# A segmented recurrence with a gated FFN: from block 2 on, token tiles of 16 steps of one batch instead of 8 steps of both

## The chip, the cores and the metric

The kernel runs on one core of a Trainium2 chip. A core has TensorE (PE: matrix products; its weight loads are shown apart as PEld), VectorE (DVE), ScalarE (ACT), GpSimd (POOL), and SyncE (SP), which here only issues transfers; 16 DMA engines move data between HBM and the on-chip memory SBUF. Engines run their own instruction streams in order and wait for each other by semaphores. The metric is device microseconds of one launch, lower is better, as the median of several runs.

## The reference

Two layers over x of shape (2 batches, 1024 steps, 512), each with a layer norm before and after and a residual:

```python
u = einsum('bsd,hd->bsh', layernorm(x), W_in) + b_in          # 512 -> 1024
s[t] = tanh(u[t] + s[t-1] * gamma + beta)                     # over 1024 steps, per channel
x = x + layernorm(einsum('bsh,dh->bsd', s, W_out) + b_out)
h = layernorm(x)
f = silu((h @ fp8(gate_w)) * gate_scale) * ((h @ fp8(up_w)) * up_scale)     # 512 -> 1536
x = x + layernorm((f @ fp8(down_w)) * down_scale)
```

fp8() rounds a weight to 8-bit floating point; the products themselves are of float32 values.

## The kernel before, in words

**Tiling of the recurrence.** The 1024 steps of a batch are cut into G = 8 segments of L = 128 steps that run side by side: with B = 2 batches that is GB = 16 columns for each of NH = 8 groups of 128 hidden channels, so one step of the recurrence is an operation on 128 partitions x 128 columns. A segment starts from a state that a warm-up finds: before the main pass, the last WARM = 96 steps of every segment are run from an arbitrary start, and the state at their end becomes the start (s0) of the *next* segment. The last column of the 16, the last segment of batch 1, has no next segment, and the warm-up leaves it out: WB = 15 columns, 120 per step. (The last segment of batch 0 is also warmed up and its result not used.) At the end `verdict` compares the states that the main pass reached with those that the warm-up had found; if they differ, or a weight's sum isn't finite, `sequential` computes everything again; otherwise the last two output tiles are stored.

**Blocks and tiles.** The 128 steps of a segment are cut into NB = 8 blocks of K = 16 steps. A block has 256 tokens, in two tiles of 128 tokens: TT = 8 steps of all 16 columns, in the order (step, batch, segment). `x_tok` and `out_tok` give this order in HBM; a load or store of a tile has the access pattern 8 x 16 x 512 there, in rows of 2 KB. The u of a block lies in `us[k]`, shape [128, NH, 16 steps, 16 columns], and the states are written over it in place.

**First stage** (lines 265 to 365). The order of blocks is 2 to 7, then 0 and 1; the number in this order is n. For each block: load x (`load_x`, line 154; the first two tiles in halves over the SP and ACT queues), statistics and norm on VectorE (`stat` 192, `norm` 199), transposes on TensorE (`trans_x`, 130), copies out of PSUM (`copy_x` 211), eight u products (`mm_u` 218), and their evacuation with bias on ScalarE (`evac_u` 227). The order on each engine is written out by hand. While the products of block n+1 run, the steps of block n run: `warm_step` for blocks 2 to 7 (n < 6), `main_step` for blocks 0 and 1. A warm-up step is coef x state (L246), + u (L247), both on VectorE, and a tanh on ScalarE (L249); a main step is L260, L261 and L262. Between them VectorE does one filler operation per step: norm, statistics, a copy, or the expansion of a quantized weight (L183). The last warm step copies its state into s0, one copy per batch (L255).

**Second stage** (lines 369 on). For a tile of 128 tokens, `mm_y` (L384) multiplies the states with W_out, then come the layer norm and residual (`y_in`, `y_resid`, `y_norm`), transposes, the gate and up products (`mm_g`, L433), silu and product (`gate`, `f_in`), the down product (`down`, L462), the layer norm and the store (`o_in`, `o_stat`, `o_out`). The loop runs over blocks k and 12 chunks fc of the FFN's inner width. While block k is in the FFN, the y products of block k+1 run at fc = 1 and fc = 4, and the 16 main steps of block k+2 are dealt out over the fc by the table STEPS. `load_r` (line 376) loads x again for the residual, behind the stores on the SP queue. `verdict` (lines 497 to 515) is called once at k = 6, fc = 7: a memset (L501), a comparison per batch (L505), reductions, a small matmul `pf` (L512), and the flag. The last two tiles' stores are the ones behind the flag's branch (L633).

Of the kernel before, what the change touches and what calls it, by code (L numbers as in the profile page):

```python
# [9 lines left out]
F32 = mybir.dt.float32  # L10
# [3 lines left out]
AF = mybir.ActivationFunctionType  # L14
ALU = mybir.AluOpType
AX = mybir.AxisListType
PSUM = bass.MemoryType.PSUM

P = 128
# [8 lines left out]
G = 8  # L28
# [4 lines left out]
def segmented(  # L33
# [21 lines left out]
    nc = tc.nc  # L55
    B, S, D = x.shape
    H = w_in.shape[1]
    I = gate_w.shape[1]
    ND, NH, NI = D // P, H // P, I // P
    L = S // G  # L60
    GB = G * B
    WB = GB - 1
    TT = P // GB
    K = 2 * TT
    N = K * GB
    NB = L // K

    x_tok = x.rearrange("b (g s) d -> s (b g) d", g=G)
    out_tok = out.rearrange("b (g s) d -> s (b g) d", g=G)

    const = ctx.enter_context(tc.tile_pool(name="const", bufs=1))
    weights = ctx.enter_context(tc.tile_pool(name="weights", bufs=1))
    states = ctx.enter_context(tc.tile_pool(name="states", bufs=1))
    small = ctx.enter_context(tc.tile_pool(name="small", bufs=4))
# [10 lines left out]
    hid = const.tile([P, 3, NH], F32, name="hid")  # L85
    ident = const.tile([P, P], F32, name="ident")
    mhalf = const.tile([P, 1], F32, name="mhalf")
    bias_u = const.tile([P, NH], F32, name="bias_u")
    coef = const.tile([P, NH, GB], F32, name="coef")
    coefw = const.tile([P, NH, WB], F32, name="coefw")  # L90
    ones = const.tile([P, 1], F32, name="ones")
    ffs = const.tile([P, 2, NI], F32, name="ffs")
    bout_bc = const.tile([P, D], F32, name="bout_bc")
# [13 lines left out]

    def constants_hid():
        nc.vector.tensor_tensor(bias_u, hid[:, 0, :], hid[:, 1, :], ALU.add)
        nc.vector.tensor_copy(coef, hid[:, 2, :].unsqueeze(2).broadcast_to([P, NH, GB]))  # L110
        nc.vector.tensor_copy(coefw, hid[:, 2, :].unsqueeze(2).broadcast_to([P, NH, WB]))


    def stats(src):
# [16 lines left out]

    us = {}

# [7 lines left out]
    order = list(range(first, NB)) + list(range(first))  # L144
    held = {}
    win_sb = win_p.tile([P, ND, H], F32, name="win_sb")

    def load_x(n, j, queues=(nc.sync,)):
        i = 2 * order[n] + j
        x_t = held["x", n, j] = xp.tile([P, D], F32, tag="x", name=f"x_{i}")  # L150
        w = D // len(queues)
        for h, queue in enumerate(queues):
            at = slice(h * w, (h + 1) * w)
            queue.dma_start(out=x_t[:, at], in_=x_tok[i * TT : (i + 1) * TT, :, at])

    def load_win(i):
        at = slice(i * H // 4, (i + 1) * H // 4)
# [54 lines left out]

    def mm_u(n, hc):
        if hc == 0:
            us[order[n]] = states.tile([P, NH, K, GB], F32, name=f"us_{n}")
        pu = held["u", n, hc] = ps_g.tile([P, 2, N], F32, tag="pg", name=f"pu_{n}_{hc}")
        for dc in range(ND):
            nc.tensor.matmul(  # L218
                pu[:, 0, :],
                lhsT=win_sb[:, dc, hc * P : (hc + 1) * P],  # L220
                rhs=held["xT", n][:, dc, :],
                start=(dc == 0),
                stop=(dc == ND - 1),
            )

    def evac_u(n, hc):
        nc.scalar.activation(  # L227
            us[order[n]][:, hc],
            held["u", n, hc][:, 0, :].rearrange("p (t q) -> p t q", t=K),
            AF.Identity,  # L230
            bias=bias_u[:, hc : hc + 1],
        )


    run = {"state": None}
    kept = []
    s0 = const.tile([P, NH, GB], F32, name="s0")
    nc.gpsimd.memset(s0.rearrange("p h (b g) -> p h b g", b=B)[:, :, :, 0], 0.0)

    def warm_step(k, t, last):  # L240
        z = small.tile([P, NH, WB], F32, tag="zw", name=f"zw_{k}_{t}", bufs=2)
        u = us[k][:, :, t, 0:WB]
        if run["state"] is None:
            z = u
        else:
            nc.vector.tensor_tensor(z, coefw, run["state"], ALU.mult)  # L246
            nc.vector.tensor_tensor(z, z, u, ALU.add)  # L247
        s = small.tile([P, NH, WB], F32, tag="sw", name=f"sw_{k}_{t}", bufs=2)
        nc.scalar.activation(s, z, AF.Tanh)  # L249
        run["state"] = s  # L250
        if last:

            for b in range(B):
                q = slice(b * G, (b + 1) * G - 1)
                nc.vector.tensor_copy(s0[:, :, b * G + 1 : (b + 1) * G], s[:, :, q])  # L255
            run["state"] = s0

    def main_step(k, t):
        z = small.tile([P, NH, GB], F32, tag="z", name=f"z_{k}_{t}", bufs=2)
        nc.vector.tensor_tensor(z, coef, run["state"], ALU.mult)  # L260
        nc.vector.tensor_tensor(z, z, us[k][:, :, t], ALU.add)  # L261
        nc.scalar.activation(us[k][:, :, t], z, AF.Tanh)  # L262
        run["state"] = us[k][:, :, t]

    def step(n, t):
        if n < WARM // K:
# [4 lines left out]

    both = (nc.sync, nc.scalar)
    load_x(0, 0, both)
    load_x(0, 1, both)
    nc.scalar.dma_start(out=hid, in_=per_hidden)
    nc.sync.dma_start(out=ffs, in_=per_ffn)
    load_win(0)
    load_win(1)
    load_x(1, 0)
    load_x(1, 1)  # L280
    load_win(2)
# [15 lines left out]
    for j in range(2):  # L297
        copy_x(0, j, 0, scalar=True)
        copy_x(0, j, 1)
    constants_hid()  # L300
    for j in range(2):
        for h in range(2):
            stat(1, j, h)
    for hc in range(NH):
        mm_u(0, hc)
        if hc in (4, 5):
            trans_x(1, hc - 4)
        if hc == 0:
            for j in range(2):
                for h in range(2):  # L310
                    norm(1, j, h)
        if hc in (5, 6):
            for h in range(2):
                copy_x(1, hc - 5, h)
        if hc == 6:
            for j in range(2):
                for h in range(2):
                    stat(2, j, h)
        evac_u(0, hc)
        if hc in (4, 5, 6):  # L320
            quant(hc - 4)
            expand(hc - 4)
            load_w(hc - 1)
# [7 lines left out]
    for n in range(NB - 1):  # L331
        mine = []
        for t in range(K):
# [26 lines left out]
            if n in (1, 2, 3, 4) and t == 9:  # L360
                c = slice((n - 1) * NH // 4, n * NH // 4)
# [11 lines left out]

    def load_r(i):
        held["x", i] = xr.tile([P, D], F32, tag="xr", name=f"xr_{i}")
        nc.sync.dma_start(out=held["x", i], in_=x_tok[i * TT : (i + 1) * TT])


    def mm_y(i, part=range(NH)):
        k, t0 = i // 2, (i % 2) * TT  # L380
        if part[0] == 0:
            held["py", i] = ps_y.tile([P, D], F32, tag="py", name=f"py_{i}")
        for hc in part:
            nc.tensor.matmul(  # L384
                held["py", i],
                lhsT=us[k][:, hc, t0 : t0 + TT, :].rearrange("p t q -> p (t q)"),
                rhs=wout_sb[:, hc, :],
                start=(hc == 0),
                stop=(hc == NH - 1),
            )  # L390
# [86 lines left out]
    def o_out(i):  # L477
        m, r = held["omr", i]
        o = held["o", i]
        c = small.tile([P, 1], F32, tag="cc", name=f"cc_{i}")  # L480
        nc.vector.scalar_tensor_tensor(c, m, r, held["c", i], ALU.mult, ALU.add)
        nc.vector.scalar_tensor_tensor(o, o, r, held["x", i], ALU.mult, ALU.add)
        nc.vector.tensor_scalar(o, o, c, None, ALU.subtract)
        dst = out_tok[i * TT : (i + 1) * TT]
        if i < 2 * NB - 2:
            nc.sync.dma_start(out=dst, in_=o)
        else:
            kept.append((dst, o))
# [8 lines left out]
    def verdict():  # L497


        bad = small.tile([P, NH, GB], F32, tag="bad", name="bad", bufs=1)  # L500
        nc.vector.memset(bad, 0.0)  # L501
        ends = us[NB - 1][:, :, K - 1, :]
        for b in range(B):
            q = slice(b * G, (b + 1) * G - 1)
            nc.vector.tensor_tensor(bad[:, :, q], ends[:, :, q], s0[:, :, b * G + 1 : (b + 1) * G], ALU.not_equal)  # L505
        bad2 = small.tile([P, 2], F32, tag="bad2", name="bad2", bufs=1)
        nc.vector.tensor_reduce(bad2[:, 0:1], bad, AX.XY, ALU.max)
        off = small.tile([P, n_sums], F32, tag="off", name="off", bufs=1)
        nc.vector.tensor_scalar(off, sums, 0.0, 0.0, ALU.mult, ALU.not_equal)
        nc.vector.tensor_reduce(bad2[:, 1:2], off, AX.X, ALU.max)  # L510
        pf = ps_t.tile([P, ND, P], F32, tag="pt", name="pf")
        nc.tensor.matmul(pf[0:1, 0, 0:2], lhsT=ones, rhs=bad2, start=True, stop=True)  # L512
        n = small.tile([1, 1], F32, tag="n", name="n", bufs=1)
        nc.vector.tensor_reduce(n, pf[0:1, 0, 0:2], AX.X, ALU.add)
        nc.vector.tensor_copy(flag, n)


    for i in range(4):
        load_r(i)
    for i in range(2):  # L520
        mm_y(i)
    n = NB - 1
# [22 lines left out]
    for i in range(last + 3):  # L545
        k, fc = divmod(i, NI)
        more = k + 1 < NB
        steps = iter(())
        if k + 2 < NB:
            t0 = sum(sum(STEPS.get(c, ())) for c in range(fc))  # L550
# [38 lines left out]
        ends = [2 * k - 2, 2 * k - 1] if k else []  # L589
# [12 lines left out]
        if more and fc == 1 and k:  # L602
            for j in range(2):
                load_r(2 * k + 2 + j)
# [396 lines left out]
```

## Time and profile before

| | |
|---|---|
| median of 3 runs | 543.51 us (543.43 to 544.18) |
| profiled execution | 543.2 us; its span in the trace 541.4 us |
| mean granted TensorE clock | 0.993 |
| busy: PE, PEld, DVE, ACT, POOL | 515.2, 408.6, 360.3, 225.4, 55.7 us |
| chain that ended last, by engine | PE 66%, DVE 19%, ACT 8%, issue 3%, DMA 1%, POOL 1% |
| first warm-up step | 28.54 us |
| copies into s0, end of the warm-up | 126.93 us |
| first y product of the second stage's chain | 161.69 us |
| last store issued | 535.40 us |

All times in the trace are microseconds from the start of the span, and nanoseconds where a mean of one instruction is given. "L218" is line 218 of the kernel. A group line reads: line, engine, operation, output<-inputs, shape, number | busy time, mean of one | idle time of the engine just ahead of these instructions, and what ended it. The chain that ended last is followed back from the last instruction, at each step to what released it; it shows which work set the end. A window row reads: stretch and length, then busy time and number of instructions of PE, PEld, DVE, ACT and POOL, the clock granted to TensorE, the mean busy share of the 16 DMA engines, and GB/s. A busy TensorE is not TensorE at its peak, since matmuls are pipelined.

### The profile page before, as it was taken

Reading aid. Unit: us, or ns where it says so; the run is one execution under the profiler, and the core shown is the slowest. Engines: PE = TensorE matmul, PEld = TensorE weight load, DVE = VectorE, ACT = ScalarE, POOL = GpSimd, SP = SyncE. Lnnn points to the kernel's source line nnn. Section 1 sums busy time; section 2 is a strip of 40 time slices with the busy share of each in tenths; the row PEclk is TensorE's granted clock in tenths of the full one; section 3 lists DMA queues with packets and bytes.
Section 4 is the critical chain, followed back from the end, with each engine's and each line's share of the span. In section 5 each row is a group of like instructions: output and inputs, shape, how many; then the busy total and the mean of one; then the engine's idle time right before and its main releaser. Section 6 shows DMA issues by size and latency. Waiting matters only on the chain.

```text
span 541.4 us, 8064 instructions
## 1 busy us (share of the span) xinstructions
PE 515.2 (95%) x2818; PEld 408.6 (75%) x2818; DVE 360.3 (67%) x1017; ACT 225.4 (42%) x590; POOL 55.7 (10%) x152
## 2 busy tenths in 40 slices
PE   3999999999999899999999999999999999999991
PEld 2888877776547787789669777966987796689990
DVE  3488888886675767765856775585677657364634
ACT  1366666665423453335225333522533351123330
POOL 1111110010011111110110111010101101110101
PEclk9999999999999999999999999999999999999997
DMA  7653545332000000200200020011002001100101
GB/s 185 181 187 110 159 153 156 118 89 87 21 1 2 0 1 0 79 2 0 46 32 1 2 78 1 1 31 49 0 2 79 1 1 28 50 1 1 41 1 44
DMA packets 15808, 27.36 MB, mean 51 GB/s; under 512 B 1424, under 2 KB 3984, under 8 KB 15760
## 3 DMA queue, kind: packets, MB, share of 16 engines
q1 hardware_dynamic: 15344, 26.49, 16.7%
q8 instruction: 24, 0.39, 0.3%
q10 hardware_dynamic: 416, 0.27, 0.2%
q14 instruction: 24, 0.20, 0.1%
HBM read 22.57 MB, written 4.19 MB: 49 GB/s over the span
## 4 chain that ended last, share of the span: by engine, by line
PE 66%; DVE 19%; ACT 8%; issue 3%; DMA 1%; POOL 1%; ACTq 0%; DVEq 0%; POOLq 0%
PE pg L433 30%; PE py L384 17%; PE pd L462 15%; DVE zw L247 5%; ACT sw L249 5%; DVE zw L246 5%; PE pu L218 3%; DVE z L261 2%; DVE z L260 2%; ACT us L262 2%; PE ph L130 1%; DMA x<-in_x_dram 1%; DVE st L116 1%; DVE st L192 1%; DVE mv L121 1%
## 5 line engine op out<-in xcount | busy, mean ns | idle before, releaser
L218 PE MATMUL pu<-xT,win_sb 128*128 128x256 f32 x512 | 123.2, 391 | 2.3 <-ACT xT L211 0.5
L218 PEld LDWEIGHTS pu<-xT,win_sb 128*128 128x128 f32 x512 | 95.1, 193 | 26.3 <-ACT us L227 13.8
L384 PE MATMUL py<-wout_sb,us 128*128 128x512 f32 x256 | 112.4, 592 | 1.0 <-DVE y L394 1.0
L433 PE MATMUL pg<-hT,gate_sb 128*128 128x256 f32 x384 | 100.6, 297 | 0.0
L433 PE MATMUL pg<-hL,gate_sb 128*128 128x256 f32 x384 | 93.9, 280 | 0.0
L433 PE MATMUL pg<-hL,up_sb 128*128 128x256 f32 x384 | 93.3, 279 | 0.0
L433 PE MATMUL pg<-hT,up_sb 128*128 128x256 f32 x384 | 93.2, 278 | 0.0
L447 DVE SCALAR_TENSOR_TENSOR f<-pg,ffs,gate 128x256 f32<-128x256 f32 x96 | 46.1, 481 | 68.2 <-ACT gate L443 68.2
L384 PEld LDWEIGHTS py<-wout_sb,us 128*128 128x128 f32 x256 | 48.4, 190 | 56.4 <-issue 54.1
L262 ACT ACTIVATE us<-z 128x128 f32<-128x128 f32 x128 | 39.7, 310 | 101.4 <-DVE z L261 99.1
L462 PE MATMUL pd<-down_sb,fL 128*128 128x512 f32 x192 | 75.9, 395 | 1.9 <-DVE fL L455 1.8
L433 PEld LDWEIGHTS pg<-hT,gate_sb 128*128 128x128 f32 x384 | 72.4, 189 | 6.1 <-issue 3.1
L433 PEld LDWEIGHTS pg<-hL,gate_sb 128*128 128x128 f32 x384 | 72.3, 188 | 5.8 <-issue 2.9
L462 PE MATMUL pd<-down_sb,fH 128*128 128x512 f32 x192 | 76.1, 396 | 0.0
L451 ACT CAST fH<-f 128x256 fp32r<-128x256 f32 x96 | 39.0, 407 | 80.7 <-DVE f L447 80.1
L433 PEld LDWEIGHTS pg<-hT,up_sb 128*128 128x128 f32 x384 | 72.5, 189 | 0.0
L433 PEld LDWEIGHTS pg<-hL,up_sb 128*128 128x128 f32 x384 | 72.3, 188 | 0.0
L443 ACT ACTIVATE gate<-pg,ffs 128x256 f32<-128x256 f32 x96 | 44.9, 468 | 59.8 <-PE pg L433 55.5
L123 POOL TENSOR_SCALAR var<-mv 128x1 f32<-128x1 f32 x64 | 14.2, 223 | 471.1 <-DVE mv L121 470.3
L455 DVE TENSOR_TENSOR fL<-f,fH 128x256 fp32r<-128x256 f32 x96 | 40.2, 418 | 10.9 <-ACT fH L451 10.3
L260 DVE TENSOR_TENSOR z<-coef,us 128x128 f32<-128x128 f32 x127 | 36.3, 286 | 12.2 <-ACT us L262 12.0
L249 ACT ACTIVATE sw<-zw 128x120 f32<-128x120 f32 x95 | 28.8, 303 | 34.4 <-DVE zw L247 34.3
(69 smaller groups left out, 508.8 us busy)
## 6 DMA issues: line engine op xcount, KB each, us to landing
xr<-in_x_dram SPq DMA_DIRECT2D x16, 256.0 KB
out_dram<-o SPq DMA_DIRECT2D x16, 256.0 KB
x<-in_x_dram SPq DMA_DIRECT2D x14, 256.0 KB
ws<-in_gate_w_dram SPq DMA_DIRECT2D x12, 256.0 KB
ws<-in_up_w_dram SPq DMA_DIRECT2D x12, 256.0 KB
ws<-in_down_w_dram SPq DMA_DIRECT2D x12, 256.0 KB
win_sb<-in_w_in_dram SPq DMA_DIRECT2D x4, 512.0 KB
wout_sb<-in_w_out_dram SPq DMA_DIRECT2D x4, 512.0 KB
```

The source lines that it names most:

```text
L218: nc.tensor.matmul(pu[:, 0, :], lhsT=win_sb[:, dc, hc * P : (hc + 1) * P], rhs=held["xT", n][:, dc, :], start=(dc == 0), stop=(dc == ND - 1),)
L246: nc.vector.tensor_tensor(z, coefw, run["state"], ALU.mult)
L249: nc.scalar.activation(s, z, AF.Tanh)
L260: nc.vector.tensor_tensor(z, coef, run["state"], ALU.mult)
L262: nc.scalar.activation(us[k][:, :, t], z, AF.Tanh)
L384: nc.tensor.matmul(held["py", i], lhsT=us[k][:, hc, t0 : t0 + TT, :].rearrange("p t q -> p (t q)"), rhs=wout_sb[:, hc, :], start=(hc == 0) ...
L433: nc.tensor.matmul(pg[:, n, :], lhsT=w[:, dc, fc * P : (fc + 1) * P], rhs=held[part, k][:, dc, :], start=(dc == 0 and part == "hT"), stop= ...
L443: nc.scalar.activation(g, held["g", i][:, 0, :], AF.Silu, scale=ffs[:, 0, i % NI : i % NI + 1])
L447: nc.vector.scalar_tensor_tensor(f, held["g", i][:, 1, :], ffs[:, 1, i % NI : i % NI + 1], held["gate", i], ALU.mult, ALU.mult)
L451: nc.scalar.copy(fH, f)
L455: nc.vector.tensor_tensor(fL, held["f", i], held["fH", i].bitcast(F32), ALU.subtract)
L462: nc.tensor.matmul(held["d", 2 * k + j], lhsT=held[part, i][:, j * P : (j + 1) * P], rhs=down_sb[:, fc, :], start=(fc == 0 and part == "fH ...
```

## The change

Blocks 0 and 1 stay as they are (`halved(k)`). In blocks 2 to 7 a tile is all 16 steps of the block of one batch: tile j is batch j, in the order (step, segment). The access pattern in HBM is then 16 x 8 x 512, again in rows of 2 KB. `us[k]` of these blocks is [128, NH, B, K, G], so that a tile's 128 tokens still lie side by side for the y product (`of_tile`), and a step (`at_step`) is 16 runs of 8 columns where it was 8 runs of 16. A y product of these blocks reads states of all 16 steps of the block; before, tile 0 read the first 8 and tile 1 the last 8.

The warm-up leaves out the last segment of each batch: WG = 7 segments, 2 x 7 x 8 = 112 columns per step instead of 120. The copy into s0 becomes one instruction instead of two; in the verdict a memset and two comparisons become one comparison. The constants, the scratch tiles and the step functions take the shape [128, NH, B, G or WG]. The instructions and their order on every engine are otherwise the same; in the compiled program the transposes of x and the first two y products wait for one more event of TensorE's own.

```diff
-    WB = GB - 1
+    WG = G - 1
...
-    x_tok = x.rearrange("b (g s) d -> s (b g) d", g=G)
-    out_tok = out.rearrange("b (g s) d -> s (b g) d", g=G)
+    def halved(k):
+        return k < 2
+    def tokens(t, i):
+        k, j = divmod(i, 2)
+        if halved(k):
+            return t.rearrange("b (g s) d -> s (b g) d", g=G)[i * TT : (i + 1) * TT]
+        return t[j].rearrange("(g s) d -> s g d", g=G)[k * K : (k + 1) * K]
...
+    def at_step(k, t):
+        return us[k][:, :, t] if halved(k) else us[k][:, :, :, t]
+    def of_tile(i, hc):
+        k, j = divmod(i, 2)
+        if halved(k):
+            return us[k][:, hc, j * TT : (j + 1) * TT].rearrange("p t b g -> p (t b g)")
+        return us[k][:, hc, j].rearrange("p t g -> p (t g)")
...
-            queue.dma_start(out=x_t[:, at], in_=x_tok[i * TT : (i + 1) * TT, :, at])
+            queue.dma_start(out=x_t[:, at], in_=tokens(x, i)[:, :, at])
...
-            us[order[n]] = states.tile([P, NH, K, GB], F32, name=f"us_{n}")
+            k = order[n]
+            us[k] = states.tile([P, NH, K, B, G] if halved(k) else [P, NH, B, K, G], F32, name=f"us_{n}")
...
     def warm_step(k, t, last):
-        z = small.tile([P, NH, WB], F32, tag="zw", name=f"zw_{k}_{t}", bufs=2)
-        u = us[k][:, :, t, 0:WB]
+        z = small.tile([P, NH, B, WG], F32, tag="zw", name=f"zw_{k}_{t}", bufs=2)
+        u = at_step(k, t)[:, :, :, 0:WG]
...
         if last:
-            for b in range(B):
-                q = slice(b * G, (b + 1) * G - 1)
-                nc.vector.tensor_copy(s0[:, :, b * G + 1 : (b + 1) * G], s[:, :, q])
+            nc.vector.tensor_copy(s0[:, :, :, 1:G], s)
             run["state"] = s0
...
     def main_step(k, t):
-        z = small.tile([P, NH, GB], F32, tag="z", name=f"z_{k}_{t}", bufs=2)
+        z = small.tile([P, NH, B, G], F32, tag="z", name=f"z_{k}_{t}", bufs=2)
         nc.vector.tensor_tensor(z, coef, run["state"], ALU.mult)
-        nc.vector.tensor_tensor(z, z, us[k][:, :, t], ALU.add)
-        nc.scalar.activation(us[k][:, :, t], z, AF.Tanh)
-        run["state"] = us[k][:, :, t]
+        u = run["state"] = at_step(k, t)
+        nc.vector.tensor_tensor(z, z, u, ALU.add)
+        nc.scalar.activation(u, z, AF.Tanh)
...
-        nc.sync.dma_start(out=held["x", i], in_=x_tok[i * TT : (i + 1) * TT])
+        nc.sync.dma_start(out=held["x", i], in_=tokens(x, i))
...
-                lhsT=us[k][:, hc, t0 : t0 + TT, :].rearrange("p t q -> p (t q)"),
+                lhsT=of_tile(i, hc),
...
-        dst = out_tok[i * TT : (i + 1) * TT]
+        dst = tokens(out, i)
...
     def verdict():
-        bad = small.tile([P, NH, GB], F32, tag="bad", name="bad", bufs=1)
-        nc.vector.memset(bad, 0.0)
-        ends = us[NB - 1][:, :, K - 1, :]
-        for b in range(B):
-            q = slice(b * G, (b + 1) * G - 1)
-            nc.vector.tensor_tensor(bad[:, :, q], ends[:, :, q], s0[:, :, b * G + 1 : (b + 1) * G], ALU.not_equal)
+        bad = small.tile([P, NH, B, WG], F32, tag="bad", name="bad", bufs=1)
+        nc.vector.tensor_tensor(bad, at_step(NB - 1, K - 1)[:, :, :, 0:WG], s0[:, :, :, 1:G], ALU.not_equal)
```

More of the change, by code (lines that the diff above doesn't have):

```diff
@@ L88, in segmented @@
     bias_u = const.tile([P, NH], F32, name="bias_u")
-    coef = const.tile([P, NH, GB], F32, name="coef")
-    coefw = const.tile([P, NH, WB], F32, name="coefw")
+    coef = const.tile([P, NH, B, G], F32, name="coef")
+    coefw = const.tile([P, NH, B, WG], F32, name="coefw")
     ones = const.tile([P, 1], F32, name="ones")
@@ L109, in constants_hid @@
         nc.vector.tensor_tensor(bias_u, hid[:, 0, :], hid[:, 1, :], ALU.add)
-        nc.vector.tensor_copy(coef, hid[:, 2, :].unsqueeze(2).broadcast_to([P, NH, GB]))
-        nc.vector.tensor_copy(coefw, hid[:, 2, :].unsqueeze(2).broadcast_to([P, NH, WB]))
+        for c in (coef, coefw):
+            c = c.rearrange("p h b g -> p h (b g)")
+            nc.vector.tensor_copy(c, hid[:, 2, :].unsqueeze(2).broadcast_to(c.shape))
     def stats(src):
@@ L227, in evac_u @@
         nc.scalar.activation(
-            us[order[n]][:, hc],
-            held["u", n, hc][:, 0, :].rearrange("p (t q) -> p t q", t=K),
+            us[order[n]][:, hc].rearrange("p a b g -> p (a b g)"),
+            held["u", n, hc][:, 0, :],
             AF.Identity,
@@ L236, in segmented @@
     kept = []
-    s0 = const.tile([P, NH, GB], F32, name="s0")
-    nc.gpsimd.memset(s0.rearrange("p h (b g) -> p h b g", b=B)[:, :, :, 0], 0.0)
+    s0 = const.tile([P, NH, B, G], F32, name="s0")
+    nc.gpsimd.memset(s0[:, :, :, 0], 0.0)
     def warm_step(k, t, last):
-        z = small.tile([P, NH, WB], F32, tag="zw", name=f"zw_{k}_{t}", bufs=2)
-        u = us[k][:, :, t, 0:WB]
+        z = small.tile([P, NH, B, WG], F32, tag="zw", name=f"zw_{k}_{t}", bufs=2)
+        u = at_step(k, t)[:, :, :, 0:WG]
         if run["state"] is None:
@@ L247, in warm_step @@
             nc.vector.tensor_tensor(z, z, u, ALU.add)
-        s = small.tile([P, NH, WB], F32, tag="sw", name=f"sw_{k}_{t}", bufs=2)
+        s = small.tile([P, NH, B, WG], F32, tag="sw", name=f"sw_{k}_{t}", bufs=2)
         nc.scalar.activation(s, z, AF.Tanh)
@@ L375, in load_r @@
         held["x", i] = xr.tile([P, D], F32, tag="xr", name=f"xr_{i}")
-        nc.sync.dma_start(out=held["x", i], in_=x_tok[i * TT : (i + 1) * TT])
+        nc.sync.dma_start(out=held["x", i], in_=tokens(x, i))
     def mm_y(i, part=range(NH)):
-        k, t0 = i // 2, (i % 2) * TT
         if part[0] == 0:
@@ L497, in verdict @@
     def verdict():
-        bad = small.tile([P, NH, GB], F32, tag="bad", name="bad", bufs=1)
-        nc.vector.memset(bad, 0.0)
-        ends = us[NB - 1][:, :, K - 1, :]
-        for b in range(B):
-            q = slice(b * G, (b + 1) * G - 1)
-            nc.vector.tensor_tensor(bad[:, :, q], ends[:, :, q], s0[:, :, b * G + 1 : (b + 1) * G], ALU.not_equal)
+        bad = small.tile([P, NH, B, WG], F32, tag="bad", name="bad", bufs=1)
+        nc.vector.tensor_tensor(bad, at_step(NB - 1, K - 1)[:, :, :, 0:WG], s0[:, :, :, 1:G], ALU.not_equal)
         bad2 = small.tile([P, 2], F32, tag="bad2", name="bad2", bufs=1)
-        nc.vector.tensor_reduce(bad2[:, 0:1], bad, AX.XY, ALU.max)
+        nc.vector.tensor_reduce(bad2[:, 0:1], bad.rearrange("p h b g -> p (h b g)"), AX.X, ALU.max)
         off = small.tile([P, n_sums], F32, tag="off", name="off", bufs=1)
```

## The prediction

> **What bounds the kernel now.** I read the chain of work that ended last first. Over the whole span it is two thirds TensorE, but cut into windows it shows four stages with four limits. To 28.5 us it goes through one load of x, its layer norm, and then TensorE alone:
>
> ```profile
> 1.97 5.01 DMA x<-in_x_dram
> 7.00 0.44 DVE st L192
> ...
> 8.72 0.42 DVE x L199
> 9.15 0.04 issue
> 9.19 1.13 PE px L130 x4
> 10.34 0.38 ACT xT L211
> 10.73 0.04 issue
> 10.77 11.17 PE pu L218 x40
> ```
>
> (start, duration, what). Every microsecond by which that load lands sooner moves TensorE's start, until the chain in front of it is bound elsewhere. From 28.54 to 126.93 us the chain is only the warm-up recurrence, 96 steps of two VectorE operations (L246, L247) and one tanh (L249): 98.4 us, 1.03 us a step. Beside them TensorE looks full, but it spends 11.5 us waiting for ScalarE to empty PSUM, so it is not the limit. Blocks 0 and 1 follow with the same recurrence 128 columns wide, and from about 190 us on TensorE runs without a gap to 530 us. Last come the final layer norm and two stores, whose data moves from about 535 to 540 us.
>
> The groups of instructions, with shapes kept apart (busy us, mean ns of one), price a step:
>
> ```profile
> L262 ACT ACTIVATE us<-z 128x128 f32<-128x128 f32 x128 | 39.7, 310 | 101.4 <-DVE z L261 99.1
> L261 DVE TENSOR_TENSOR z<-z,us 128x128 f32<-128x128 f32 x128 | 37.5, 293 | 4.5
> L260 DVE TENSOR_TENSOR z<-coef,us 128x128 f32<-128x128 f32 x127 | 36.3, 286 | 12.2 <-ACT us L262 12.0
> L249 ACT ACTIVATE sw<-zw 128x120 f32<-128x120 f32 x95 | 28.8, 303 | 34.4 <-DVE zw L247 34.3
> L247 DVE TENSOR_TENSOR zw<-zw,us 128x120 f32<-128x120 f32 x95 | 26.9, 283 | 3.6
> L246 DVE TENSOR_TENSOR zw<-coefw,sw 128x120 f32<-128x120 f32 x95 | 26.4, 278 | 8.7 <-ACT sw L249 1.3
> L505 DVE TENSOR_TENSOR bad<-us,s 128x56 f32<-128x56 f32 x2 | 0.3, 214 | 0.0
> ```
>
> The windows of busy time show at the head a stretch in which only loads of x are left, and near the end the two stores (the two columns before the last are the granted clock and the DMA engines' busy share; the last is GB/s):
>
> ```profile
> 16.00:17.00 1.00, 1.00 (x6) 0.90 (x5) 0.97 (x5) 0.20 (x1) 0.12 (x1) 1.00 1.02 348
> 19.00:20.00 1.00, 1.00 (x6) 0.90 (x5) 0.00 (x0) 0.00 (x0) 0.00 (x0) 1.00 0.53 170
> 536.00:537.00 1.00, 0.00 (x0) 0.00 (x0) 0.00 (x0) 0.00 (x0) 0.00 (x0) 0.50 0.42 113
> 537.00:538.00 1.00, 0.00 (x0) 0.00 (x0) 0.00 (x0) 0.00 (x0) 0.00 (x0) 0.50 0.49 156
> 538.00:539.00 1.00, 0.00 (x0) 0.00 (x0) 0.00 (x0) 0.00 (x0) 0.00 (x0) 0.50 0.46 139
> ```
>
> At 19 us and in the tail the share stops near one half, at 16 us, where weights load too, it reaches 1.02 at twice the rate.
>
> **The warm-up steps, 120 to 112 columns.** From 128 to 120 columns the rows fall by 286-278 = 8, 293-283 = 10 and 310-303 = 7 ns, 25 ns for eight columns. The change takes away eight more, and all three operations lie on the path. Against it: the operand u of L247 is now cut into 16 runs of 7 words, where it had 8 runs of 15. The Trainium skill (Vector Engine (DVE) Microarchitecture Reference, "Measured stream behaviour on trn2") states that a port keeps full rate only on adjacent pairs of words that start on an 8-byte boundary, and that an isolated word costs about 0.65 cycle. An odd run ends in one such word, so by the rule (my estimate) eight more of them cost 8 x 0.68 = 5.4 ns a step. The row beside it is L505: 56 columns in 8 runs of 7 on all three operands took 214 ns; a line through the 8-column bias_u add (156 ns) and the 128-column L260 (286 ns) puts 56 columns at 208, so 6 ns for 8 runs. The row doesn't contradict the rule, and it excludes a price several times higher. By rows alone I would gain 25 ns, with the rule 20; I take 21. Ten steps hold a bn_stats and bn_aggr pair, where VectorE and not the tanh is late; they gain about the VectorE part, 13 to 18. Sum: 95 x 21 ns = 2.0 us, bounds 1.1 (double the rule's price for the runs, and nothing on the ten steps) and 2.4. Next late in an ordinary step would be the filler operation on VectorE (norm, copy or expand, 0.41 us): it ends some 0.07 us before the tanh and gets earlier together with it, so it doesn't take over.
>
> **The handover and the verdict.** The two 56-column copies into s0 (188 ns each, 0.29 us together) become one of 112 columns, about 0.22: 0.1 gained, on the path. In the verdict a memset (0.15 us on the chain) and two comparisons (0.36) become one of 112 columns (about 0.27). That is 0.25 us, and TensorE is waiting for it:
>
> ```profile
> 482.39 0.19 PE L512 MATMUL pf<-bad,ones 128*1 128x2 f32 x2 [0.40 <-DVE bad L510]
> ```
>
> Its wait is 0.40 us, so all 0.25 count. Together 0.35 us, bounds 0.1 and 0.5.
>
> **Loads and stores.** The first load is block 2, which changes; so do the last two stores (block 7). Bytes and 2 KB rows stay; only the DRAM side's outer dimension goes from 8 to 16. The Trainium skill (DMA: Bandwidth & Descriptors, "Why a DMA increments its semaphore by 16 and not by 1") says that a transfer uses the largest number of engines up to 16 that divides the slowest dimension of both sides: 8 before, 16 after. The trace agrees in the shares of about 0.5. No row shows a 16-engine store of these bytes; a 16-engine mix of loads is the 348 GB/s row, against 170 GB/s with x alone. By the rule the moving halves; by the rows only what is not start-up and landing latency can halve.
>
> Head: 512 KB of x move in about 2.3 to 4.5 us, and the first tile lands at 4.98 (its first VectorE statistic), the second at 7.00. At double rate I put the first at about 4.2 and the second near 5. VectorE then needs two tiles of statistics, aggregates and the first norm: from the first landing to the second tile's norm about 3.0 us when nothing waits (0.75 + 0.25 + 0.75 + 0.25 to the second aggregate, then 1.05 as now from 7.67 to 8.72). That gives 7.2 to 7.5 in place of 8.72. I take 1.3 us; bounds 0 (both tiles land by latency alone, or the weights, now behind x on all engines, land last) and 1.7. TensorE then runs the same 17 us earlier, as its next inputs do; the x tiles of later blocks are prefetched far ahead and change nothing.
>
> Tail: store 1 is issued at 533.96, store 2 at 535.40 when its layer norm ends. Their 524 KB move from 535.0 to 540.1, of which some 0.9 us is ramp, so 2.1 us a store. With twice the engines the second is bound by its own issue: 535.40 + 1.05 (issue to first data, as for store 1) + 0.9 + 1.05 = 538.4, a gain of 1.7. The writing side may not scale fully, so I take 1.5; bounds 0 and 2.6 (no ramp).
>
> **The steps of blocks 2 to 7 in the late stage.** ScalarE writes and VectorE reads 16 runs of 8 words now, all pairs: no lone word. They lie beside a TensorE without gaps after 190 us, and cost nothing. In 170 to 190 us VectorE is late and TensorE idles; 16 steps of block 2 lie there: at 3 to 5 ns for each of some 30 operations, 0.1 us; bounds 0 and 0.2.
>
> **A wait that is new.** A y matmul of a tile read 8 steps of a block; it now needs all 16. Behind it on TensorE stand the gate matmuls, and everything waits for those. The tightest place is block 2:
>
> ```profile
> 206.96 0.31 ACT L262 ACTIVATE us<-z 128x128 f32<-128x128 f32 x1 [0.69 <-DVE z L261]
> 210.69 0.41 PEld L384 LDWEIGHTS py<-wout_sb,us 128*128 128x128 f32 x2
> ```
>
> The first is that block's last tanh, done at 207.27, 3.4 us ahead of the matmul's weights (block 3: 5.4). Nothing above makes the steps 3.4 us later, so it costs 0. Blocks 0 and 1, whose y has no such cover, keep the old tiles. The transposes of x and two y matmuls also wait for one more TensorE event of their own, long past; at worst 12 drained pipelines, under the 11.5 us that TensorE idles in the warm-up. On SP the queue's order is unchanged.
>
> **Sum.** 2.0 + 0.35 + 1.3 + 1.5 - 0.1 = 5.05 us. The profiled execution took 543.2 us (span 541.4, 1.8 around it), the median of the runs is 543.51; the gain is 0.93% of either, and I count from the median: 538.4 us.
>
> **Rivals.** *Transfers bound by latency* (chance 0.15): the spread over engines brings nothing at either end. For it: a first microsecond of the stores at 51 GB/s, and 8 engines that may already be the writing side's limit. Against it: 170 and 348 GB/s. Then 2.35 - 0.1 = 2.25 us, 541.3. *One end only* (0.20): head or tail stays, 539.7 to 539.9. *Short runs* (0.03), the slower side: each restart of a run costs VectorE c ns at L247, 95 times, with eight more runs: 95 x 8c. The warm-up's gain is gone at c = 2.8, and the kernel is slower beyond c = 6.8; at 10 ns it would be 7.6 us against gains of 5.2, 545.9. L505 shows about 0.8 ns a run. *No change* (0.05): both transfers stay and the runs eat half of the steps' gain, 543.
>
> **Chances and range.** The likeliest case (0.57) has 536.5 to 539.3 as its own range. The upper end reaches past one end only into the latency case, the lower to the sum of the upper bounds: 2.4 + 0.5 + 1.7 + 2.6 = 7.2, 536.3. So 536.3 to 541.2. A measurement here can tell 0.2% (1.1 us) from no change: faster 0.92, same 0.05, slower 0.03.
>
> **What would show it.** L246, L247 and L249 at 112 columns near 270, 276 and 296 ns and a step of about 1.01 us; the first gate of TensorE, the transpose now at 9.19, near 8; tail windows with a share well above 0.5 and the second store's data ending near 538.5; pf's wait under 0.2 us; no wait of the y matmuls for L262's successor. It would be wrong if L247 doesn't get shorter, if the share stays at one half, or if TensorE's first u matmul waits for win_sb.

## The result and the profile after

| | before | after |
|---|---|---|
| median (9 runs each) | 543.43 us (542.29 to 544.23) | 541.65 us (541.10 to 542.36) |
| ratio to before | | 0.9973, interval 0.9963 to 0.9983 |
| profiled execution; its span | 543.2; 541.4 us | 541.67; 539.8 us |
| mean granted TensorE clock | 0.993 | 0.996 |
| first warm-up step | 28.54 us | 26.64 us |
| first y product of the second stage's chain | 161.69 us | 157.65 us |
| last matmul ends | 529.90 us | 530.16 us |

The kernel is faster by 0.27%, where 0.93% was forecast: 541.65 us against 538.4, and outside the range of 536.3 to 541.2. The table already says where to look. The change is 4.0 us ahead when the second stage begins, and 0.26 us *behind* when TensorE ends. What lies between is the second stage, whose matmuls have the same shapes and order as before.

First the parts that went as expected. The head, from the timeline of the kernel after (start, duration, engine, line, output<-inputs, and in brackets the idle time ahead with what ended it):

```profile
4.04 0.75 DVE L214 BATCH_NORM_STATS2 st<-x 128x6 f32<-128x256 f32 x2 [3.19 <-DMA x<-in_x_dram]
7.95 0.71 PEld L141 LDWEIGHTS px<-ident,x 128*128 128x128 f32 x4 [0.47 <-DVE x L221]
9.52 10.51 PE L241 MATMUL pu<-xT,win_sb 128*128 128x256 f32 x40 [0.46 <-ACT xT L233]
26.64 0.30 ACT L272 ACTIVATE sw<-us 128x112 f32<-128x112 f32 x1
```

The first tile of x is there at 4.04 us instead of 4.98, the transposes that stood at 9.19 start at 7.95, and the u products run from 9.52 instead of 10.77. So the spread of the load over engines is worth 1.25 us up to here. Another 0.66 us comes in the u products themselves (10.51 us for the first 40 instead of 11.17). That part can't be put down to the change. In every profile the early ones of these products start 427 ns apart and the later ones 216 ns. The slow spacing lasts for nine products in the profile of before and for six in this one; in the other profiles with the new loads, where these products are the same, it lasts for three (e10) to eleven (e12), and the 40 take 9.90 to 11.48 us. The granted clock reads 1.00 there in the kernels before and after; what ends the slow stretch is not settled.

The groups of instructions answer to the rows of a warm-up step:

```profile
L282 DVE TENSOR_TENSOR z<-z,us 128x128 f32<-128x128 f32 x128 | 37.5, 293 | 4.5
L272 ACT ACTIVATE sw<-zw 128x112 f32<-128x112 f32 x95 | 28.2, 297 | 32.9 <-DVE zw L270 32.7
L270 DVE TENSOR_TENSOR zw<-zw,us 128x112 f32<-128x112 f32 x95 | 26.1, 275 | 3.6
L269 DVE TENSOR_TENSOR zw<-coefw,sw 128x112 f32<-128x112 f32 x95 | 25.7, 270 | 8.2 <-ACT sw L272 1.3
```

L246, L247 and L249 (now L269, L270 and L272) went from 278, 283 and 303 ns to 270, 275 and 297: 22 ns a step. The first line is the main step's add: 293 ns as before, though its operand lies in short runs in 96 of the 128 (those 96 alone: 293.5 before, 293.6 after).

The handover into the main pass, the first y product of the second stage, and the verdict's matmul, again from the timeline:

```profile
122.92 0.22 DVE L275 COPY s<-sw 128x112 f32<-128x112 f32 x1 [0.42 <-ACT sw L272]
157.65 5.39 PE L403 MATMUL py<-wout_sb,us 128*128 128x512 f32 x12 [1.04 <-DVE y L413]
481.86 0.19 PE L527 MATMUL pf<-bad,ones 128*1 128x2 f32 x2
```

One copy of 0.22 us stands for two of 0.29 together, and `pf`, which used to wait 0.40 us for `bad`, waits for VectorE no more; in part because TensorE now comes to it later (in e7 below, where TensorE is as fast as before, 0.08 us of idle time is left). The tail, in windows of busy time:

```profile
536.00:537.00 1.00, 0.00 (x0) 0.00 (x0) 0.00 (x0) 0.00 (x0) 0.00 (x0) 0.50 0.57 191
537.00:538.00 1.00, 0.00 (x0) 0.00 (x0) 0.00 (x0) 0.00 (x0) 0.00 (x0) 0.50 0.87 229
538.00:539.00 1.00, 0.00 (x0) 0.00 (x0) 0.00 (x0) 0.00 (x0) 0.00 (x0) 0.50 0.02 8
```

The DMA share rises to 0.87 and the rate to 229 GB/s, where they had stopped at 0.49 and 156; nearly all data is out by 538 us. From the last matmul's end to the end of the span it is 9.6 us instead of 11.5.

And now the second stage. A gate or up matmul has a slice of the weights as its stationary operand, which is loaded first (PEld), and `hT` or `hL`, the rounded part and the remainder of the transposed h, as its moving operand, which is streamed against it. TensorE's timeline for the first and last `up` matmul of one chunk, and the matmul after them, of the kernel before:

```profile
245.50 0.28 PE L433 MATMUL pg<-hT,up_sb 128*128 128x256 f32 x1
...
246.29 0.28 PE L433 MATMUL pg<-hL,up_sb 128*128 128x256 f32 x1
246.40 0.39 PE L462 MATMUL pd<-down_sb,fH 128*128 128x512 f32 x1
```

and of the kernel after:

```profile
242.32 0.28 PE L452 MATMUL pg<-hT,up_sb 128*128 128x256 f32 x1
...
243.16 0.28 PE L452 MATMUL pg<-hL,up_sb 128*128 128x256 f32 x1
243.28 0.40 PE L481 MATMUL pd<-down_sb,fH 128*128 128x512 f32 x1
```

The column of durations says 0.28 us in both, since a matmul's end is modelled. It is the distance of the *starts* that tells the pace: eight matmuls from 245.50 to 246.40, 113 ns each, against 242.32 to 243.28, 120 ns each. Over all chunks after 200 us, the kernel before alternates between 113.3 and 117.9 ns from one chunk to the next (mean 115.6), and the kernel after keeps to 119.8. The same shows in the y products of two consecutive blocks, before:

```profile
258.90 7.03 PE L384 MATMUL py<-wout_sb,us 128*128 128x512 f32 x16
306.89 7.03 PE L384 MATMUL py<-wout_sb,us 128*128 128x512 f32 x16
```

and after:

```profile
255.99 7.03 PE L403 MATMUL py<-wout_sb,us 128*128 128x512 f32 x16
304.63 7.03 PE L403 MATMUL py<-wout_sb,us 128*128 128x512 f32 x16
```

A block takes 48.64 us instead of 47.99. The slow pace holds to the end: after 480 us, when no step of the recurrence is left (the last ends at 444.8 us), the up matmuls still start 119.7 ns apart, against 115.6 before. The y products themselves still start 429.0 ns, and the u products 216 ns, from one another. Adding up the distances from each start to the next, as means of the five blocks from the second y products on, shows where the loss lies: of 0.63 us a block, 0.40 are in the up matmuls, 0.17 in the gate matmuls and 0.06 in the down matmuls. All three have the same shapes, operands and order as before.

### The profile page after: what moved, and what is told of

It reads as the page before. It is cut to its first block, busy times and chain, and to the rows that moved or that the text cites. A ratio compares the mean times of both kernels' runs of the same rounds, so it can differ in the third digit from the quotient of the medians.

```text
span 539.8 us, 8063 instructions
## 1 busy us (share of the span) xinstructions
PE 518.4 (96%) x2818; PEld 413.0 (77%) x2818; DVE 357.9 (66%) x1014; ACT 225.0 (42%) x590; POOL 55.3 (10%) x152
## 5 line engine op out<-in xcount | busy, mean ns | idle before, releaser
L241 PE MATMUL pu<-xT,win_sb 128*128 128x256 f32 x512 | 121.4, 388 | 1.3 <-ACT xT L233 0.5
L452 PE MATMUL pg<-hT,gate_sb 128*128 128x256 f32 x384 | 101.8, 298 | 0.0
L452 PE MATMUL pg<-hL,up_sb 128*128 128x256 f32 x384 | 96.3, 283 | 0.0
L452 PE MATMUL pg<-hT,up_sb 128*128 128x256 f32 x384 | 96.1, 283 | 0.0
L452 PE MATMUL pg<-hL,gate_sb 128*128 128x256 f32 x384 | 95.4, 281 | 0.0
L452 PEld LDWEIGHTS pg<-hL,up_sb 128*128 128x128 f32 x384 | 73.5, 191 | 0.0
L481 PEld LDWEIGHTS pd<-down_sb,fL 128*128 128x128 f32 x192 | 36.4, 190 | 7.4 <-DVE fL L474 2.8
```

The lines of the kernel that those rows point to most:

```text
L241: nc.tensor.matmul(pu[:, 0, :], lhsT=win_sb[:, dc, hc * P : (hc + 1) * P], rhs=held["xT", n][:, dc, :], start=(dc == 0), stop=(dc == ND - 1),)
L452: nc.tensor.matmul(pg[:, n, :], lhsT=w[:, dc, fc * P : (fc + 1) * P], rhs=held[part, k][:, dc, :], start=(dc == 0 and part == "hT"), stop= ...
L481: nc.tensor.matmul(held["d", 2 * k + j], lhsT=held[part, i][:, j * P : (j + 1) * P], rhs=down_sb[:, fc, :], start=(fc == 0 and part == "fH ...
```

## The experiments

**Where it could come from.** The smaller tiles shift everything allocated behind them. The allocation of the compiled program (no part of the profile) has `gate_sb` 32 bytes lower in each partition, because `coefw` has shrunk from 480 to 448 bytes, and `hT` 224 bytes lower, because `zw`, `sw` and `bad` shrank too. All operands of the second stage started on a multiple of 64 bytes before, and start 32 bytes off one now. My first theory was that alignment. The rivals were the short runs of the steps in VectorE and ScalarE, the additional TensorE events, and the transfers. All kernels here keep the work of the kernel they start from, unless said, and add a tile that nothing uses.

In the tables, `up` is the mean distance from one start to the next within the eight up matmuls of a chunk, over all chunks after 200 us; a block is the distance between the y products of successive blocks.

**e1_aligned, e2_before_shifted.** Alignment restored in the kernel after, and taken from the kernel before, with the same line behind `coefw`:

```diff
+    const.tile([P, 8], F32, name="pad_const")
```

> The changed kernel with 32 unused bytes a partition put back behind coefw, so that gate_sb, up_sb, down_sb and the late tiles (hT, hL, fH, fL) start on a multiple of 64 bytes again, as before the change; instructions and their order are the same. Theory of addresses (TensorE's fast matmuls in the FFN run at 120 ns when their operands start 32 bytes off a 64-byte boundary, and at 113 to 118 when not): the spacing of the up matmuls falls from 120 to 118 or less, a block of the FFN from 48.64 to about 48.0 us, and the time from 541.7 to 537.3 us. Rival, the layout of the states (16 short runs per step disturb TensorE's reads): no change, 541.7. Rival, the additional TensorE events that transposes and y products wait for: no change, 541.7.

> The kernel before with an unused tile of 32 bytes a partition behind coefw, which moves the weights and the late tiles to 32 bytes off a 64-byte boundary; nothing else is changed. Theory of addresses: the FFN gets as slow as in the changed kernel, up matmuls at 120 ns, 48.6 us a block, and the time rises by some 4.4 us to 547.9. Both rivals (layout of the states, additional events): the same as before, 543.5.

**e3_late_off, e4_weights_off.** The tiles of the second stage (`hT`, `hL` and all that are allocated behind them) 32 bytes further, in e1 and in the kernel after:

```diff
+    late.enter_context(tc.tile_pool(name="pad_late", bufs=1)).tile([P, 8], F32, name="pad_late")
```

> As the first kernel (weights on 64-byte boundaries), but with 32 more unused bytes ahead of the late tiles, so that only hT, hL, f, fH and fL are 32 bytes off. If the address of the moving operand sets the pace: gate and up matmuls at 120 ns (hT and hL move), about 541.7 us. If the address of the stationary operand does: gate and up at 113 to 118 ns and only the down product, whose stationary side is fH and fL, may be slower; 537.3 to 538.

> The changed kernel with 32 unused bytes ahead of the late tiles only: gate_sb, up_sb and down_sb stay 32 bytes off a 64-byte boundary, hT, hL, fH and fL are on one. The converse of the kernel before it: if the moving operand sets the pace, gate and up fall to 113 to 118 ns and the down product, whose moving side is down_sb, stays; about 537.3 to 538 us. If the stationary one does, gate and up stay at 120 ns, 541.7.

| | median us | ratio to before | `up` spacing ns | block us |
|---|---|---|---|---|
| e1_aligned | 541.93 | 0.9974 (0.9964 to 0.9985) | 119.8 | 48.63 |
| e2_before_shifted | 542.96 | 1.0002 (0.9991 to 1.0012) | 115.6 | 48.0 |
| e3_late_off | 538.54 | 0.9916 (0.9899 to 0.9932) | 117.1 | 48.23 |
| e4_weights_off | 539.32 | 0.9934 (0.9918 to 0.9950) | 117.1 | 48.23 |

The alignment theory fell: e1 has every operand on a multiple of 64 bytes and is as slow as the kernel after, e2 has none and is as fast as the kernel before. The y products of e2:

```profile
259.32 4.88 PE L385 MATMUL py<-wout_sb,us 128*128 128x512 f32 x11
307.31 4.02 PE L385 MATMUL py<-wout_sb,us 128*128 128x512 f32 x9
```

(the records of some matmuls are missing, so the counts differ; the starts are 47.99 us apart). But e3 and e4 moved the pace although their steps, events and transfers are those of the kernel after, so none of the rivals explains it; e7 below, which has all three and the full pace of before, settles that. What e3 and e4 have in common is not where the weights lie, nor where `hT` lies, but the distance of the two: 160,544 bytes from `gate_sb` to `hT`, where it is 160,704 before (and in e2) and 160,512 after (and in e1). Modulo 256 (the remainder on division by 256) that is 32, 192 and 0. This became the second theory: the pace of these matmuls depends on the distance between stationary and moving operand. (A pad ahead of the late tiles also changes their distance to the states, the constants and all else that is allocated before them; "distance" stands for all of these.)

**e5 to e8.** The same line in the kernel after with 64, 128, 192 and 256 bytes (`[P, 16]`, `[P, 32]`, `[P, 48]`, `[P, 64]`).

> The changed kernel with 64 unused bytes a partition between the weights and the late tiles. In the first four runs the pace followed neither address by itself but their difference: 160704 bytes from gate_sb to hT gave 115.6 ns an up matmul and 48.0 us a block (before, and before with everything moved by 32), 160512 gave 119.8 and 48.63, 160544 gave 117.1 and 48.23. Theory of the distance (the difference modulo some power of two sets how far the moving and the stationary read get in each other's way): this kernel has 160576, a value not seen, and its pace lies between 113 and 120 ns; 537 to 541.7 us. Rival, chance of the program or the chip: no order in it, 119.8 ns and 541.7 us as without the gap.

> The same with 128 bytes, a distance of 160640. Theory of the distance: a pace between 113 and 120 ns, 536 to 541.7 us; if the way back to a full period is even, about that of the 192 bytes. Rival (chance): 119.8 ns, 541.7 us.

> The same with 192 bytes: exactly the distance of before, 160704, with every address other than before. Theory of the distance: the FFN of before comes back, up matmuls at 115.6 ns in alternating 113.3 and 117.9, a block in 48.0 us, and the whole gain shows: 541.7 - 7 x 0.64 = 537.2 us. Rival (chance, or absolute addresses): 119.8 ns, 541.7 us.

> The same with 256 bytes, a distance of 160768. If the period is 256 bytes or less, it is as slow as without a gap: 119.8 ns, 48.63 us a block, 541.7 us. If the period is longer, it is another pace, and with the theory of the distance between 113 and 120 ns.

**e10 to e12.** 96, 160 and 224 bytes, which neither kernel of the change had.

> The changed kernel with a gap of 96 bytes, a distance of 160608 (96 past a multiple of 256). The distance sets the pace: 0 gives 119.8 ns an up matmul, 32 117.1, 64 117.5, 128 119.4, 192 115.6. A value between 115 and 120, by the neighbours 117 to 119; 538 to 541 us. If the pace were set by the distance modulo 128, it would be 117.5 or less, as 32 is.

> The same with 160 bytes, a distance 160 past a multiple of 256. By its neighbours 128 (119.4 ns) and 192 (115.6) between 115 and 119; if the odd multiples of 32 are better than the even ones beside them, as 32 is better than 0, below 117. 537 to 541 us.

> The same with 224 bytes, a distance 224 past a multiple of 256, between 192 (115.6 ns) and 256, which is 0 again (119.7). 115 to 118 ns; 536 to 540 us. If 113.3 ns without the alternation to 117.9 is to be had, it is at this distance or at 160: a block would be at 47.5 us and the time near 534.

All distances together, with after and e4 for 0 and 32:

| distance mod 256 | kernel | median us | ratio to before | `up` ns | block us |
|---|---|---|---|---|---|
| 0 | after | 541.65 | 0.9973 (0.9963 to 0.9983) | 119.8 | 48.64 |
| 0 | e8_gap256 | 541.36 | 0.9966 (0.9949 to 0.9982) | 119.7 | 48.64 |
| 32 | e4_weights_off | 539.32 | 0.9934 (0.9918 to 0.9950) | 117.1 | 48.23 |
| 64 | e5_gap64 | 539.19 | 0.9925 (0.9907 to 0.9943) | 117.5 | 48.37 |
| 96 | e10_gap96 | 542.74 | 0.9992 (0.9982 to 1.0001) | 120.1 | 48.72 |
| 128 | e6_gap128 | 541.82 | 0.9971 (0.9961 to 0.9982) | 119.4 | 48.67 |
| 160 | e11_gap160 | 540.72 | 0.9968 (0.9952 to 0.9983) | 118.4 | 48.46 |
| 192 | e7_gap192 | 537.15 | 0.9887 (0.9866 to 0.9908) | 115.6 | 48.0 |
| 224 | e12_gap224 | 541.09 | 0.9966 (0.9954 to 0.9977) | 118.3 | 48.50 |

With the down matmul that follows counted in, e4 is at 116.8 ns and e6 at 120.1; the time of a block is the surer measure.

e7 has the distance of the kernel before, and its pace comes back in full, with the alternation between 113.3 and 117.9 ns. Its `up` matmuls in a fast chunk:

```profile
296.01 0.28 PE L453 MATMUL pg<-hT,up_sb 128*128 128x256 f32 x1
...
296.81 0.28 PE L453 MATMUL pg<-hL,up_sb 128*128 128x256 f32 x1
296.92 0.39 PE L482 MATMUL pd<-down_sb,fH 128*128 128x512 f32 x1
```

and its y products of two blocks, 47.98 us apart:

```profile
255.42 7.03 PE L404 MATMUL py<-wout_sb,us 128*128 128x512 f32 x16
303.40 7.03 PE L404 MATMUL py<-wout_sb,us 128*128 128x512 f32 x16
```

With 537.15 us e7 beats both kernels. e8 moves the late tiles further than e7 and is back at the pace of the kernel after, so it isn't the room that counts. That 0 and 256 agree is the only sign of a period of 256 bytes; no other pair of distances tests it. Within 256 there is no simple rule: 32 is among the good distances and 96 is the worst, which a period of 64 or of 128 bytes would not give. The guesses by neighbours show it too: 96 was expected at 117 to 119 ns and has 120.1, and the even 113.3 ns that was thought possible at 160 or 224 came at neither.

**e13_h192, e14_rest192.** The pad of e7 moves `hT` and `hL`, which TensorE reads in the gate and up products, together with all later tiles. e13 puts only `hT` and `hL` at e7's place, with 64 bytes more behind them so that the rest stands as in the kernel after, modulo 256; e14 leaves those two and moves the rest by 192 bytes, with a pad ahead of the pool `xr`:

```diff
+    late.enter_context(tc.tile_pool(name="pad_late", bufs=1)).tile([P, 48], F32, name="pad_late")
...
+    late.enter_context(tc.tile_pool(name="pad_rest", bufs=1)).tile([P, 16], F32, name="pad_rest")
```

(this is e13; e14 has `pad_rest` alone, with 48 elements).

> The changed kernel with 192 unused bytes ahead of hT and hL and 64 more behind them: hT and hL are 192 bytes past a multiple of 256 from the weights, all later tiles (x for the residual, y, h, gate, f, fH, fL) stand as in the changed kernel, modulo 256. If TensorE's own pair of operands in the gate and up matmuls sets their pace: 115.6 ns and some 48.0 to 48.1 us a block, about 537.4 us. If the tiles that VectorE and ScalarE read and write beside it set it: 119.8 ns, 541.7 us.

> The converse: hT and hL stand as in the changed kernel, all later tiles are moved by 192 bytes. If the gate and up matmuls' own operands set their pace: 119 to 120 ns, 48.6 us a block, 541.5 us. If the other engines' tiles set it: 115.6 ns, 537.2 us.

"Gate and up" and "down" are the distances from each start to the next added up, in us a block:

| | median us | ratio to before | `up` ns | gate and up | down | block us |
|---|---|---|---|---|---|---|
| before | 543.43 | 1 | 115.6 | 23.27 | 11.11 | 48.01 |
| after | 541.65 | 0.9973 (0.9963 to 0.9983) | 119.8 | 23.85 | 11.16 | 48.64 |
| e13_h192 | 539.64 | 0.9949 (0.9932 to 0.9966) | 117.5 | 23.53 | 11.09 | 48.25 |
| e14_rest192 | 541.14 | 0.9977 (0.9965 to 0.9990) | 119.9 | 23.91 | 10.98 | 48.53 |
| e7_gap192 | 537.15 | 0.9887 (0.9866 to 0.9908) | 115.6 | 23.24 | 11.11 | 48.0 |

The y products of two consecutive blocks, of e13 and then of e14:

```profile
255.22 7.03 PE L405 MATMUL py<-wout_sb,us 128*128 128x512 f32 x16
303.47 7.03 PE L405 MATMUL py<-wout_sb,us 128*128 128x512 f32 x16
```

```profile
255.20 7.03 PE L404 MATMUL py<-wout_sb,us 128*128 128x512 f32 x16
303.74 7.03 PE L404 MATMUL py<-wout_sb,us 128*128 128x512 f32 x16
```

Moving `hT` and `hL` alone takes the up matmuls from 119.8 to 117.5 ns (117.9 in all chunks but about one a block) and gives back 0.39 of the 0.64 us a block, 0.31 of it in gate and up. Moving all else leaves the up matmuls at 119.9 and gives back 0.11, in the down matmuls alone. So the place of the moving operand counts for about half of the loss in gate and up, and no other tile brings that half. The other half, the fast chunks of 113.3 ns, comes only when both groups are moved; which of the other tiles brings it, the two runs don't tell. The expectation that TensorE's own pair sets the whole pace, 115.6 ns in e13, did not come true.

**e9_outer8.** The other half of the account: e7 with the outer dimension 8 for all loads and stores, everything else as in e7. The tiles of blocks 2 to 7 then hold other tokens than the rest of the kernel takes them for, so it computes something else; the work is the same.

```diff
     def tokens(t, i):
-        if halved(k):
-            return t.rearrange("b (g s) d -> s (b g) d", g=G)[i * TT : (i + 1) * TT]
-        return t[j].rearrange("(g s) d -> s g d", g=G)[k * K : (k + 1) * K]
+        return t.rearrange("b (g s) d -> s (b g) d", g=G)[i * TT : (i + 1) * TT]
```

> The changed kernel with the 192 byte gap (537.15 us), and with the access pattern of before, 8 x 16 x 512, for all loads and stores: the tiles of blocks 2 to 7 then hold other tokens than the rest of the kernel takes them for, so the output is not the reference's; the work is the same. If the 16-fold outer dimension is what brought the head and the tail forward: the first warm-up step goes back from about 27 to 28.5 us, the last store takes 6.0 us from its issue to the end of the span instead of 4.1, and the time rises by 3.4 to 3.8 us to about 540.8. If the transfers brought nothing: 537.2.

Measured: 540.38 us, ratio 0.9952 (0.9938 to 0.9965), against 0.9887 (0.9866 to 0.9908) for e7. The difference of the spans is 538.5 - 535.5 = 3.0 us. The first statistic of e9:

```profile
5.02 0.75 DVE L212 BATCH_NORM_STATS2 st<-x 128x6 f32<-128x256 f32 x2 [4.17 <-DMA x<-in_x_dram]
```

and that of e7:

```profile
4.05 0.75 DVE L214 BATCH_NORM_STATS2 st<-x 128x6 f32<-128x256 f32 x2 [3.21 <-DMA x<-in_x_dram]
```

The landing is back where it was before the change, the first warm-up step comes at 28.28 us instead of 27.06, and from the last matmul to the end it is again 11.5 us instead of 9.6. So the outer dimension of the transfers is what gains at both ends: 1.2 us at the head in this pair of profiles, 1.9 at the tail. The tail is the steadier: 11.5 us in all three profiles with the outer dimension 8 (before, e2, e9), 9.6 to 9.7 in all with 16. What is left of e9 against the kernel before, 0.48% or 2.6 us (0.35% to 0.62%), is the warm-up, the handover and the verdict, for which the prediction had 2.35 less 0.1.

## Why the prediction was wrong

| step of the prediction | predicted us | measured us, after | in e7 |
|---|---|---|---|
| head | 1.3 | 1.90 (28.54 to 26.64); 1.8 between the means of all profiles with either pattern | 1.48 |
| warm-up steps | 2.0 | 2.09 (first to last tanh 98.05 to 95.96) | 2.05 |
| handover | 0.1 | 0.07 (last warm-up tanh to first main tanh 1.38 to 1.31) | 0.07 |
| verdict | 0.25 | 0.40 (the whole wait) | 0.32 |
| tail | 1.5 | 1.89 (11.51 to 9.62) | 1.90 |
| sum of these | 5.15 | 6.35 | 5.82 |
| steps of blocks 2 to 7, second stage | -0.1 | -4.71: 1.64 between the spans, less the 6.35 above | 0.04: 5.86 between the spans, less the 5.82 above |

**The step that failed** is "The steps of blocks 2 to 7 in the late stage": they "lie beside a TensorE without gaps after 190 us, and cost nothing". It is true of the steps. But the sum then took TensorE's own time there as unchanged, without a term or a reason of its own; no term and no rival had a matmul that keeps its shape and becomes slower. The up matmuls' spacing went from 115.6 to 119.8 ns because smaller tiles moved the addresses, the gate and down matmuls lost with them: 0.64 us for each of nearly eight blocks, about 4.7 us, against all gains of 6.35. e7 shows that this is the whole of it: with the distance of before, the last row of the table is nothing (0.04 us), and the kernel stands at 0.9887, 6.1 us below the kernel before (5.0 to 7.3). The prediction had 5.05, and the 537.15 us of e7 lie inside its range.

**The head** came out beyond its upper bound of 1.7. The mechanism and its size were right: 4.04 and 7.95 where 4.2 and "near 8" stood, and u products that start 1.25 us sooner (1.4 between the means of all profiles), where 1.3 was taken. The 0.66 us more came from the slow first u products, which vary by more than that from profile to profile: in the 13 profiles with the new loads the first warm-up step comes at 26.07 to 27.47 us. So part of the 1.90 is chance.

**The warm-up** was right in size and, but for the price of the runs, in mechanism. Eight more runs that end in a lone word should have cost 5.4 ns a step by the prediction's estimate from the Trainium skill (Vector Engine (DVE) Microarchitecture Reference, "Measured stream behaviour on trn2"). The section prices elements that hop one by one, and lets runs of two or more adjacent words hop freely if they start on an 8-byte boundary, as these do; that the last word of an odd run pays was the prediction's addition. The add with its runs of 7 words is 5 ns longer than the multiply beside it (275 and 270), exactly as with runs of 15 (283 and 278), so no run here shows such a price. The whole step doesn't decide it: the measured 22 ns lie between the 25 of the rows and the 20 with the price. (The lower bound of this term adds up to 1.2 us, not 1.1; nothing hangs on it.)

**The tail** gained 1.9 where 1.5 was taken: the share did go well above one half, as the prediction's rule of engines dividing the outer dimension has it. The rate did not double in any one microsecond (229 GB/s at best against 156), but the writing side did not hold it back either: the shares from 535 us on add up to 2.03 us of all sixteen engines before (0.44, 0.42, 0.49, 0.46, 0.19, 0.03) and 2.00 after (0.54, 0.57, 0.87, 0.02), so sixteen engines took no longer for a byte than eight.

**The rivals.** The time of 541.65 lies next to the 541.3 of "transfers bound by latency". It is a coincidence: both transfers gained what they were meant to, and e9 shows it. The total alone would have confirmed the wrong story; it took the stages one by one. "Short runs" is refuted by the row of 275 ns.

**What stays open.** That the two operands' reads get in each other's way in SBUF is argued only: the runs show that the pace goes with the place of the late tiles, in about half with that of `hT` and `hL`. No run moved the weights alone, without the states beside them. Why 192 is best and 96 worst, why the fast pace comes in every other chunk (from chunk to chunk the weights' slice moves on by 512 bytes, and the buffers of gate, f, fH and fL change) and only with both groups of tiles in place, and why y and u products kept their pace through all of this, is not settled. The distances 0, 32 and 192 were each met by two or more kernels, which agree; the other five were run as one kernel each.

## What to carry to other kernels

A change in a tile's size moves every tile that is allocated later, and with it possibly the pace of matmuls that the change doesn't touch. So compare, stage by stage, the starts of successive matmuls before and after, also where the instructions are the same, and don't read a total as the sum of the edits. When a tile shrinks, leave the room or add a pad so that the weights and the data of the busiest matmuls keep their distance, and try a few pads: between the best and the worst they were worth 1.1% here, about as much as the edit gains with the right one, and four times what it gained with none.

## What the runs showed that was not expected

- Matmuls of 128x128 by 128x256, with the same operands, started every 115.6 to 120.1 ns according to how far the late tiles, the moving one among them, were allocated from the stationary one, modulo 256 bytes: 119.8 (0), 117.1 (32), 117.5 (64), 120.1 (96), 119.4 (128), 118.4 (160), 115.6 (192), 118.3 (224). The granted clock was 0.993 to 0.996 in the kernels before, after and e7. The alignment of the tiles to 64 bytes made no difference (e1 against after, e2 against before, e3 against e4).
- A profile's matmul duration (0.28 us) does not show this; the starts do.
- Sixteen runs of 7 words in one operand of a VectorE add, instead of eight of 15, cost less than 1 ns: it stays 5 ns above the multiply beside it, 275 against 270 after 283 against 278.
- The outer dimension of 16 instead of 8 took the stores' rate from at most 156 to 229 GB/s in one microsecond, and the engines' share from 0.49 to 0.87, in the same sum of engine time.
- The first u products of a launch start 427 ns apart instead of 216, for three to eleven of them from profile to profile, at a granted clock that reads 1.00 (before and after).
